# The last 65 keys of an attention kernel: their values and their scores made with the keys as the moving operand

## The chip, the cores and the metric

The kernel runs on one core of a Trainium2 chip. The metric is device time in microseconds; lower is better. TensorE is called PE here, VectorE DVE, ScalarE ACT, GpSimd POOL and SyncE SP, as the profile names them. On PE a matmul has a stationary operand, which a weight load (PEld) puts into the array, and a moving operand, whose columns are streamed through it.

## The reference

A gated cross-attention block followed by a mixture of low-rank adapters, all in fp32. There are 4 batches of 256 queries with 512 features, and a context of 1601 keys with 512 features. 32 query heads share 8 key-value heads (4 query heads each), with 128 features a head.

```python
q = (query @ Wq + bq).reshape(B, L, NKV, G, HDIM)
k_, v_ = jnp.split(kv @ Wkv + bkv, 2, axis=-1)
...
scores = jnp.einsum('blkgd,bmkd->bkglm', q, k) * scale
attn = jax.nn.softmax(scores, axis=-1)
o = jnp.einsum('bkglm,bmkd->blkgd', attn, v).reshape(B, L, NHEAD * HDIM)
return o @ Wo + bo
...
x = x + jnp.tanh(g_xattn[0]) * xattn(_layernorm(x), ctx, ...)
x = x + jnp.tanh(g_ffn[0]) * ffn(_layernorm(x), ...)
```

1601 keys are 12 blocks of 128 and 65 more. The change is about those 65.

## The kernel before

**Groups.** The main loop (lines 1976 to 2028) goes over batch `b`, key-value head `h` and half `l` of the queries: 4 x 8 x 2 = 64 groups. A group has 128 queries of 4 heads, so 512 columns. Its scores are kept as keys (partitions) by 512 queries in tiles `p`, two key blocks in each: seven tiles, of which the first (`j` = 0) holds the 65 last keys alone, in the half `p[:, 0, :]`; its other half is unused. `pairs` is the list of the seven.

**Scores, softmax, values.** `score_unit` (line 1217) makes one tile's scores: for each block a matmul into one PSUM bank (line 1246, keys stationary, 512 query columns moving), an eviction by ACT (line 1255), and then `fold` (line 1169) on DVE takes the running maximum, from tile 2 on; the 65 keys enter it at line 1178. `softmax` (line 1268) spreads the maximum over the keys, subtracts it tile by tile on DVE (line 1285), takes the exponential on ACT (line 1288), and sums on DVE. `av_unit` (line 1321) multiplies a tile of exponentials by the values (line 1337), and `normalize` finishes. `run_group` (line 1783) interleaves the scores of the present group with the value products of the previous one, tile by tile.

**Projections.** Keys, values and queries of two heads at a time come from `pair_steps` (line 971), which computes 2 x 2 blocks with 7 products in place of 8. For the values, the 65 last keys are done apart by `tail` (line 1124): for each of the two heads four matmuls with the 65 context rows stationary (`rest`, 65 columns) and the weights moving (128 columns) give 65 x 128 values in PSUM, which ACT copies into the value tile `v` (line 1136). That is run for 15 of the 16 pairs; the first pair has its own code. The x steps (line 589) load and normalise the inputs of two batches and turn them for the query projection; they run once at the start and once more in the middle, for batches 2 and 3.

**Order.** The order of instructions on PE, DVE and ACT is written by the program itself. It keeps estimated clocks (`clock`) for PE ("now"), DVE and ACT, and a list of the times at which the eight PSUM banks come free (`free`, `bank`, `give`). `spend(ns)` moves PE's clock on and lets waiting pieces of DVE and ACT work start (`pump`); `vec` and `act` move theirs; `later` puts a piece into a queue; `fit` emits pieces that fit before a given time; `force` emits what something depends on. Projections are tasks with a due group (`Task`, `window`), done between the groups or in free places. All the estimated costs are numbers in the code: `mm_cost(n)`, `BLOCK_COST` = 224 ns for a 128 x 128 block, `TR_COST` = 108 ns for a transpose. DMAs are issued by SP and POOL in the order of the program.

Of the kernel before, what the change touches and what calls it, by code (L numbers as in the profile page):

```python
# [10 lines left out]
F32 = mybir.dt.float32  # L11
# [4 lines left out]
P = 128  # L16
NHEAD = 32
NKV = 8
HDIM = 128
G = NHEAD // NKV  # L20
# [7 lines left out]
def flamingo_kernel(  # L28
# [51 lines left out]
    nc = tc.nc  # L80
    B, L, D = x.shape
    LK = ctx_kv.shape[1]
    NC = D // P
# [5 lines left out]
    FULL = KT - 1 if rows[-1] < P else KT  # L89
# [4 lines left out]
    pairs = [tuple(range(i, min(i + 2, FULL))) for i in range(0, FULL, 2)]  # L94
# [6 lines left out]
    HK = FULL // 2 * P  # L101
    NSUB = -(-HK // 512)
    SUB = HK // NSUB
    REST = rows[-1] if FULL < KT else 0
# [8 lines left out]
    small = ctx.enter_context(tc.tile_pool(name="small", bufs=4))  # L113
# [4 lines left out]
    SEM = 200  # L118
# [3 lines left out]
    clock = {"now": 0.0, "v": 0.0, "a": 0.0, "hold": 0.0}  # L122
    free = [0.0] * NBANK
    done = {}
    queues = {q: deque() for q in ("sub", "oT", "so", "exp", "ln", "T", "norm", "turn", "sum", "low", "low_a")}

    def vec(ns, ready=None):

        clock["v"] = max(clock["v"], clock["now"] + SEM if ready is None else ready) + ns
        return clock["v"] + SEM  # L130

    def act(ns, ready=None):
        clock["a"] = max(clock["a"], clock["now"] + SEM if ready is None else ready) + ns
        return clock["a"] + SEM
# [58 lines left out]
    def fit(engine, until):  # L193

        while True:
            some = [
                (start_of(q[0]), i, q)
                for i, q in enumerate(queues.values())
                if q and q[0][0] == engine and start_of(q[0]) + q[0][1] <= until + FIT
            ]  # L200
            if not some:
                return
            take(min(some)[2])

    def spend(ns, ready=0.0):

        clock["now"] = max(clock["now"], ready) + ns
        pump(clock["now"])
        turn_more()

    def bank(name):
        free.remove(min(free))
        return ps.tile([P, 512], F32, tag="bank", name=name)

    give = free.append


    ident = const.tile([P, P], F32, name="ident")
# [29 lines left out]
    def mm_cost(n):  # L248

        return 2 * (max(n, P) / 1.2 + 2)  # L250

    TR_COST = 108
    BLOCK_COST = 224
# [331 lines left out]
    JOINT = 2  # L585
# [79 lines left out]
    def key_col(i):  # L665

        return HK if i == FULL else i * P + (REST if i * P >= HK else 0)
# [198 lines left out]
    qT_t, kT_t, v_t = {}, {}, {}  # L866
# [104 lines left out]
    def pair_steps(kind, b, hp, then=None):  # L971
# [4 lines left out]
        nm = f"{kind}_{b}_{hp}"  # L976
        h0 = 2 * hp
        banks = {}
        second = {}

        def a(slot, c):
            return w_t[kind, b, hp][:, slot, c, :]
# [139 lines left out]
            ]  # L1122

        def tail():
            bk = bank(f"pt{nm}")
            for f in range(2):
                for j, (cols, slot, c) in enumerate(tail_cols(f)):
                    nc.tensor.matmul(  # L1128
                        bk[:REST, f * HDIM : (f + 1) * HDIM],
                        cols,  # L1130
                        a(slot, c),
                        start=j == 0,
                        stop=j == NC - 1,
                    )
            for f in range(2):
                nc.scalar.copy(v_t[b, h0 + f][:REST, FULL], bk[:REST, f * HDIM : (f + 1) * HDIM])
                t = act(250)
            give(t)
            over()
# [19 lines left out]
        parts = [[step(i, s, n) for i in (1, 2, 6, 7, 5, 4, 3)] for s, n in cols]  # L1159
        if REST and not wide:  # L1160
            ready = [("T", "kv", b), ("w", kind, b, hp)]
            parts.append([(2 * NC * BLOCK_COST, ready, tail, True)])
        left = [sum(len(p) for p in parts)]
        return parts

# [51 lines left out]
    def score_unit(key, j):  # L1217

        b, h, l = key
        nm = "_".join(map(str, key))  # L1220
        free_p = 0.0
        if j == 0:
            p_t[key] = []
            acc_t[key] = pool.tile([P, 2, W], F32, tag="mx", name=f"mx_{nm}", bufs=1)
        if key == last and j > 0:

            if j == 1:
                flat = pool.tile([P, NC * 2 * HW], F32, tag="ctxT", name="p_last", bufs=1)
                late.extend(
                    flat[:, i * 2 * W : (i + 1) * 2 * W].rearrange("p (t w) -> p t w", t=2)  # L1230
                    for i in range(NPAIR - 1)
                )
            p = late.pop(0)
        else:

            if len(ring) >= NBUF:
                before, i = ring[-NBUF]
                free_p = force(("sum", before, max(i, min(NPAIR - FULL // 2 + 1, NPAIR - 1))))
            ring.append((key, j))
            p = pool.tile([P, 2, W], F32, tag="p", name=f"p_{nm}_{j}", bufs=NBUF)  # L1240
        p_t[key].append(p)
        for k, i in enumerate(pairs[j]):
            r = rows[i]
            spend(mm_cost(W), max(min(free), done.get(("qT", b, h), 0.0)))
            sc = bank(f"sc_{nm}_{i}")
            nc.tensor.matmul(  # L1246
                sc[:r, :],
                kT_t[b, h][:, key_col(i) : key_col(i) + r],
                qT_t[b, h][:, :, l * P : (l + 1) * P],
                start=True,  # L1250
                stop=True,
            )
            t = max(clock["now"] + SEM, free_p)
            fit("a", t)
            nc.scalar.copy(p[:r, k, :], sc[:r, :])  # L1255
            t = act(585, t)
            give(t)
        fit("v", t)
        ns = fold(acc_t[key], ALU.max, j, key)
        if ns:  # L1260
            vec(ns, t)

    acc_t, sum_t, late, ring = {}, {}, [], []
    last = (B - 1, NKV - 1, NL - 1)
# [437 lines left out]
    tasks = []  # L1702
# [273 lines left out]
    for hi, (b, h) in enumerate(heads):  # L1976
        pair, coming = (b, h // 2), next_pair(b, h // 2)
        nxt = heads[hi + 1] if hi + 1 < len(heads) else None
        for l in range(NL):
            now = hi * NL + l  # L1980
            cur = (b, h, l)
            if cur == last:
                break
            if (h, l) == (NKV - 4, 1) and b + 1 < B and (b + 1) % JOINT == 0:
                load_pair("q", b + 1, 0)
                tasks.append(Task(x_steps(b + 1), now + 7))
            swap_at["group"] = now
            run_group(cur, prev)
            if prev is not None:
                steps = out_steps(prev)  # L1990
                if steps:
                    tasks.insert(0, Task(steps, now + 1 if by_blocks(*prev[:2]) else None))
                    if by_blocks(*prev[:2]):
                        out_task[prev[:2]] = tasks[0]
            prev = cur
            if (b, h, l) == (B - 1, NKV - 3, NL - 1):
                tail_space()
                tasks.append(Task(ffn_weight_steps() + [(0, 0, early_norms)]))
                both = [ffn_steps(*t) for t in early]
                tasks[:0] = [Task(route, now + 4) for route, _ in both]  # L2000
                tasks.extend(Task(steps, spare=True) for _, steps in both)
            if nxt is not None and nxt[0] % JOINT == 0:
                tasks.append(Task(q_steps(*nxt, l), now, first=True))
            elif nxt is not None and l == 0:
                load_q(*nxt)
            if coming is not None and (h % 2, l) == (0, 1):
                cb, cp = coming
                if cb == b:
                    then = lambda c=coming: next_weights("v", *c)
                    steps = sum(pair_steps("k", cb, cp, then), [])  # L2010
                else:
                    steps = first_k_steps(cb)
                tasks.append(Task(steps, (hi | 1) * NL + (NL - 1) * (cb == b), now))
            if coming is not None and (h % 2, l) == (1, 0):
                cb, cp = coming
                follow = next_pair(cb, cp)
                then = None if follow is None else lambda f=follow: next_weights("k", *f)
                for part in pair_steps("v", cb, cp, then):
                    tasks.append(Task(part, (hi | 1) * NL + NL, now))
                if cb == b and cp == NKV // 2 - 1 and b + 1 < B:  # L2020
                    tasks.append(Task(ctx_steps(b + 1)))
            if (h, l) == (NKV - 1, NL - 1) and b + 1 < B:

                force(("T", "kv", b + 1))
                force(("w", "v", b + 1, 0))
            window(now)
            if l == NL - 1 and nxt == heads[-1]:
                load_wo(*nxt)
# [51 lines left out]
```

## Time and profile before

| | us |
|---|---|
| median of 3 runs | 2532.07 (2532.05 to 2533.65) |
| the profiled execution | 2532.2 |
| its span | 2530.4 |
| PE busy | 2521.6 |
| DVE busy | 2175.3 |
| ACT busy | 1263.6 |
| POOL busy | 208.8 |

The granted PE clock is 1.00. The groups that hold most of the time, with the number of instructions and the mean of one:

| line, engine | what | count | busy us | mean ns |
|---|---|---|---|---|
| 1246 PE | scores of full blocks | 1536 passes | 720.6 | 592 |
| 1246 PE | scores of the 65 last keys | 128 passes | 65.3 | 592 |
| 1337 PE | value products | 1640 passes | 765.5 | 592 |
| 1128 PE | values of the 65 last keys | 240 passes | 31.1 | 273 |
| 1255 ACT | evictions of scores | 820 | 478.4 | 586 |
| 1255 ACT | of these, 65 keys | 64 | 37.2 | 581 |
| 1288 ACT | exponentials | 442 | 422.3 | 990 |
| 1285 DVE | subtractions | 442 | 482.4 | 1136 |
| 1136 ACT | evictions of the values' tail | 30 | 6.4 | 262 |

An fp32 matmul appears as two weight loads and two passes. Matmul ends are modelled and neighbours overlap, so the distance between two starts, or the chain's time over its count, says what a pass costs, and the mean duration doesn't. "Idle before" is the time for which an engine had nothing to do before the instructions of a row, and behind the arrow stands what ended it.

### The profile page before, as it was taken

How to read it: one execution, taken by the hardware profiler on the slowest of the kernel's cores; microseconds unless marked ns; L12 is line 12 of the kernel's file. 1: busy time of each engine (PE TensorE's matmuls, PEld its weight loads, DVE VectorE, ACT ScalarE, POOL GpSimd, SP SyncE). 2: the span in 40 equal slices, each digit the busy share in tenths (PEclk: the TensorE clock that was granted, in tenths of full speed). 3: DMA queues.
4: the chain of work that ended last, by engine and by line, in shares of the span. 5: the costliest groups of instructions: out<-in, count | busy, mean ns of one | idle time of the engine just before them, and what ended most of it. 6: DMA issues, size and time to landing. Idle time of an engine off the chain costs nothing.

```text
span 2530.4 us, 27018 instructions
## 1 busy us (share of the span) xinstructions
PE 2521.6 (100%) x9199; PEld 1493.8 (59%) x9199; DVE 2175.3 (86%) x3323; ACT 1263.6 (50%) x2062; POOL 208.8 (8%) x271
## 2 busy tenths in 40 slices
PE   9999999999999999999999999999999999999999
PEld 7557566565555656555665565756656565555544
DVE  4999898898899989999878887878788888889886
ACT  2545454545455554555545454545455455555551
POOL 1000000001001000110010000000000100000100
PEclk9999999999999999999999999999999999999999
DMA  5646857669666543224255535455532222221211
GB/s 170 143 92 130 146 123 118 151 110 246 80 92 99 85 81 74 71 71 152 58 98 100 98 77 96 109 81 110 154 80 65 82 54 67 67 63 44 71 34 50
DMA packets 300136, 246.24 MB, mean 97 GB/s; under 512 B 180533, under 2 KB 256341, under 8 KB 296158
## 3 DMA queue, kind: packets, MB, share of 16 engines
q1 hardware_dynamic: 267278, 211.71, 36.6%
q0 software_dynamic: 32192, 32.55, 8.8%
q8 instruction: 72, 1.18, 0.2%
q14 instruction: 66, 0.54, 0.1%
q10 hardware_dynamic: 528, 0.26, 0.0%
HBM read 147.96 MB, written 96.49 MB: 97 GB/s over the span
## 4 chain that ended last, share of the span: by engine, by line
PE 98%; DVE 1%; DMA 0%; ACT 0%; issue 0%; SPq 0%; ACTq 0%
PE sc L1246 28%; PE av L1337 27%; PE pxv L1015 6%; PE pxk L1004 6%; PE pxq L1004 4%; PE pox L472 4%; PE pyv L1015 3%; PE pyk L1004 3%; PE pyq L1004 2%; PE poy L472 2%; PE pzv L1015 2%; PE pzk L1004 2%; PE pzq L1004 1%; PE ptv L1128 1%; PE poz L472 1%; PE py L1581 1%
## 5 line engine op out<-in xcount | busy, mean ns | idle before, releaser
L1246 PE MATMUL sc<-qT,kT 128*128 128x512 f32 (+1 forms) x1664 | 775.9, 592 | 0.0
L1337 PE MATMUL av<-p,v 65*128 65x512 f32 x1640 | 765.5, 592 | 0.5 <-ACT p L1288 0.5
L1255 ACT COPY p<-sc 65x512 f32<-65x512 f32 x820 | 478.4, 586 | 572.8 <-PE sc L1246 549.0
L1337 PEld LDWEIGHTS av<-p,v 65*128 65x128 f32 x1640 | 311.2, 190 | 384.3 <-issue 380.1
L1246 PEld LDWEIGHTS sc<-qT,kT 128*128 128x128 f32 (+1 forms) x1664 | 308.1, 186 | 375.6 <-issue 349.5
L1285 DVE TENSOR_TENSOR p<-p,mb 65x512 f32<-65x512 f32 x442 | 482.4, 1136 | 0.3
L1288 ACT ACTIVATE p<-p 65x512 f32<-65x512 f32 x442 | 422.3, 990 | 31.0 <-DVE p L1285 29.7
L1181 DVE TENSOR_TENSOR mx<-mx,p 128x1024 f32<-128x1024 f32 x252 | 308.1, 1223 | 146.3 <-ACT p L1255 141.7
L478 POOL DMA_DIRECT2D kept_x<-po x210 | 182.6, 925 | 2039.8 <-ACT po L477 1864.4
L1181 DVE TENSOR_TENSOR sm<-sm,p 128x1024 f32<-128x1024 f32 x252 | 307.6, 1221 | 42.0 <-ACT p L1288 32.0
L1004 PE MATMUL pxq<-xq,wq 128*128 128x256 f32 x512 | 131.2, 379 | 0.0
L1049 ACT ACTIVATE kT<-pxk,biasT 128x384 f32<-128x384 f32 (+1 forms) x120 | 58.1, 509 | 126.5 <-PE pxk L1004 126.0
L1004 PEld LDWEIGHTS pxq<-xq,wq 128*128 128x128 f32 x512 | 92.4, 189 | 32.1 <-issue 15.8
L1049 ACT ACTIVATE qT<-pxq,biasT 128x256 f32<-128x256 f32 x64 | 30.4, 474 | 148.8 <-PE pxq L1004 148.8
L1175 DVE TENSOR_TENSOR mx<-p,p 128x1024 f32<-128x1024 f32 x63 | 76.9, 1221 | 31.6 <-ACT p L1255 31.4
L1004 PE MATMUL pxk<-T,wk 128*128 128x417 f32 (+1 forms) x240 | 90.4, 499 | 0.0
L1015 PE MATMUL pxv<-wv,ctxT 128*128 128x128 f32 x720 | 90.2, 275 | 0.0
L1015 PE MATMUL pxv<-wv,T 128*128 128x128 f32 x720 | 90.2, 275 | 0.0
L1004 PE MATMUL pxk<-ctxT,wk 128*128 128x417 f32 (+1 forms) x240 | 90.0, 499 | 0.0
L1015 PEld LDWEIGHTS pxv<-wv,ctxT 128*128 128x128 f32 x720 | 86.4, 192 | 4.2 <-issue 3.8
L1015 PEld LDWEIGHTS pxv<-wv,T 128*128 128x128 f32 x720 | 86.4, 192 | 4.2 <-issue 3.8
L1052 ACT COPY v<-pxv 128x384 f32<-128x384 f32 x90 | 43.0, 478 | 83.4 <-PE pxv L1015 83.1
(273 smaller groups left out, 2779.5 us busy)
## 6 DMA issues: line engine op xcount, KB each, us to landing
kept_x<-po POOLq DMA_DIRECT2D x210, 128.0 KB, 4.8
wo<-kept_wo SPq DMA_DIRECT2D x22, 1024.0 KB, 7.8
kept_q<-wq SPq DMA_DIRECT2D x16, 896.0 KB, 4.3
wq<-kept_q SPq DMA_DIRECT2D x16, 896.0 KB, 5.1
space<-kept_wo SPq DMA_DIRECT2D x22, 512.0 KB, 3.9
wk<-kept_k SPq DMA_DIRECT2D x11, 896.0 KB, 4.8
wv<-kept_v SPq DMA_DIRECT2D x11, 896.0 KB, 4.6
ctxT<-kept_ctx SPq DMA_DIRECT2D x12, 801.0 KB, 11.8
```

Of the source, the lines that this page charges most:

```text
L472: nc.tensor.matmul(bk[:, :HD], left[i]()[:, c, :], blk[:, c, :], start=first and c == 0, stop=c == 1, skip_group_check=True,)
L478: nc.gpsimd.dma_start(x2_kept[b, l, d], part, accum_op=ALU.add)
L1004: nc.tensor.matmul(bk[:, :n], a(SLOT[i], c), operand(i, c, s, n), start=first and c == 0, stop=c == 1, skip_group_check=True,)
L1015: nc.tensor.matmul(bk[:, t * HDIM : (t + 1) * HDIM], operand(i, c, s + t * P, P), a(SLOT[i], c), start=first and t == 0 and c == 0, stop=c ...
L1049: nc.scalar.activation(dst, src, AF.Identity, bias=bias_of(kind, h0 + f))
L1175: nc.vector.tensor_tensor(acc, p[first], p[first + 1], op)
L1181: nc.vector.tensor_tensor(acc, acc, p[j], op)
L1246: nc.tensor.matmul(sc[:r, :], kT_t[b, h][:, key_col(i) : key_col(i) + r], qT_t[b, h][:, :, l * P : (l + 1) * P], start=True, stop=True,)
L1255: nc.scalar.copy(p[:r, k, :], sc[:r, :])
L1285: nc.vector.tensor_tensor(p, p, m, ALU.subtract)
L1288: nc.scalar.activation(p, p, AF.Exp, scale=scale)
L1337: nc.tensor.matmul(av, v_t[b, h][:r, i, :], p_t[key][j][:r, k, :], start=(j == 0 and k == 0), stop=(j == NPAIR - 1 and k == len(pairs[j]) ...
```

## The change

It has three parts.

1. *Values.* `tail` now makes the weights stationary (128 columns) and the 65 context rows moving, so that PSUM holds 128 features x 65 keys for each of the two heads. ACT copies both into a new tile `vr` (128 x 130). A new step, `tail_turn`, transposes the two on PE into 65 x 128 and ACT copies these into `v` as before. The planner's cost for the tail's products goes from 224 to 124 ns each.
2. *Scores.* For tile 0, `score_unit` calls the new `score_rest`. Four matmuls, one for each query head, have the 128 queries stationary and the 65 keys moving; the result is 128 queries x 4 x 65 keys in one bank. DVE turns it in blocks of 32 x 32 out of PSUM into the unused half of the tile: the first 64 keys with one instruction, the last key, repeated 32 times, with another. ACT then places the blocks in twelve copies: for each of four strips of 32 queries two copies of 32 keys and one copy of the last key. These copies are emitted when the next tile's two evictions have been emitted. The rest of the softmax is as before.
3. *x steps.* For batches 2 and 3 they start when head 5 has reached its second half, in place of head 4, and are due 4 groups later in place of 7. Their loads move with them.

```diff
         def tail():
-            bk = bank(f"pt{nm}")
+            banks["t"] = bk = bank(f"pt{nm}")
             for f in range(2):
                 for j, (cols, slot, c) in enumerate(tail_cols(f)):
                     nc.tensor.matmul(
-                        bk[:REST, f * HDIM : (f + 1) * HDIM],
+                        bk[:, f * REST : (f + 1) * REST],
+                        a(slot, c),
                         cols,
-                        a(slot, c),
                         start=j == 0,
                         stop=j == NC - 1,
                     )
+            second["t"] = small.tile([P, 2 * REST], F32, tag="vr", name=f"vr_{nm}", bufs=1)
+            nc.scalar.copy(second["t"], bk[:, : 2 * REST])
+            done[nm, "t"] = act(230)
+            over()
+
+        def tail_turn():
+            bk = banks["t"]
             for f in range(2):
-                nc.scalar.copy(v_t[b, h0 + f][:REST, FULL], bk[:REST, f * HDIM : (f + 1) * HDIM])
+                nc.tensor.transpose(
+                    bk[:REST, (2 + f) * HDIM : (3 + f) * HDIM], second["t"][:, f * REST : (f + 1) * REST], ident
+                )
+            for f in range(2):
+                nc.scalar.copy(
+                    v_t[b, h0 + f][:REST, FULL], bk[:REST, (2 + f) * HDIM : (3 + f) * HDIM]
+                )
                 t = act(250)
             give(t)
             over()
...
-            parts.append([(2 * NC * BLOCK_COST, ready, tail, True)])
+            parts.append([(2 * NC * 124, ready, tail, True), (2 * TR_COST, (nm, "t"), tail_turn)])
...
         p_t[key].append(p)
+        if pairs[j] == (FULL,):
+            score_rest(key, p, free_p)
+            return
...
             give(t)
+        if key in turned:
+            t = turned.pop(key)(t)
         fit("v", t)
...
+    turned = {}
+
+    def score_rest(key, p, free_p):
+
+        b, h, l = key
+        assert REST == 65
+        spend(G * 2 * 62, max(min(free), done.get(("qT", b, h), 0.0)))
+        sc = bank(f"sr_{'_'.join(map(str, key))}")
+        for g in range(G):
+            nc.tensor.matmul(
+                sc[:, g * REST : (g + 1) * REST],
+                qT_t[b, h][:, g, l * P : (l + 1) * P],
+                kT_t[b, h][:, HK : HK + REST],
+                start=True,
+                stop=True,
+            )
+        by_key = sc[:, : G * REST].rearrange("p (g k) -> p g k", k=REST)
+        two = p[:, 1, : 2 * P].rearrange("p (g k) -> p g k", k=64)
+        one = p[:, 1, 2 * P : 3 * P].rearrange("p (g k) -> p g k", k=32)
+        t = max(clock["now"] + SEM, free_p)
+        fit("v", t)
+        nc.vector.transpose(two, by_key[:, :, :64])
+        nc.vector.transpose(one, by_key[:, :, 64:65].to_broadcast([P, G, 32]))
+        give(vec(600, t))
+        t = clock["v"] + SEM
+
+        def place(after):
+            dst = p[:, 0, :].rearrange("p (g q) -> p g q", g=G)
+            for a in range(4):
+                q, k = slice(32 * a, 32 * a + 32), 32 * a
+                for c in range(2):
+                    nc.scalar.copy(dst[32 * c : 32 * c + 32, :, q], two[q, :, 32 * c : 32 * c + 32])
+                nc.scalar.copy(dst[64:65, :, q], one[k : k + 1])
+            return max(after, act(12 * 220, t))
+
+        turned[key] = place
...
-            if (h, l) == (NKV - 4, 1) and b + 1 < B and (b + 1) % JOINT == 0:
+            if (h, l) == (5, 1) and b + 1 < B and (b + 1) % JOINT == 0:
                 load_pair("q", b + 1, 0)
-                tasks.append(Task(x_steps(b + 1), now + 7))
+                tasks.append(Task(x_steps(b + 1), now + 4))
```

## The prediction

> **What bounds the kernel now.** I read the page's busy times first, then the chain that ended last, then the groups with shapes kept apart, and then short stretches of chain and timeline.
>
> ```profile
> span 2530.4 us, 27018 instructions
> PE 2521.6 (100%) x9199; PEld 1493.8 (59%) x9199; DVE 2175.3 (86%) x3323; ACT 1263.6 (50%) x2062; POOL 208.8 (8%) x271
> PE 98%; DVE 1%; DMA 0%; ACT 0%; issue 0%; SPq 0%; ACTq 0%
> ```
>
> TensorE is never without work: 2521.6 of 2530.4 us, and the chain is 98% PE. A gain must come out of PE's own time; ScalarE (half idle) and VectorE (14% idle) can be loaded further until they make PE wait. So the question is what a PE pass costs. Every fp32 matmul stands in the trace as two weight loads and two passes. These rows are from the chain in two short stretches, and from the groups by shape:
>
> ```profile
> 246.87 1.75 PE ptv L1128 x16
> 1257.44 1.34 PE pxv L1015 x12
> L1246 PE MATMUL sc<-qT,kT 128*65 128x512 f32 x128 | 65.3, 592 | 0.0
> L1015 PEld LDWEIGHTS pxv<-wv,ctxT 128*128 128x128 f32 x720 | 86.4, 192 | 4.2 <-issue 3.8
> L1128 PEld LDWEIGHTS ptv<-wv,rest 128*65 128x65 f32 x180 | 20.1, 138 | 0.0
> ```
>
> Both products move 128 columns. With 65 stationary columns a pass takes 1.75/16 = 109 ns, with 128 it takes 1.34/12 = 112 ns. So at 128 x 128 it is no longer the moving operand that sets the pace but the weight load, which takes 54 ns more for 63 more columns (192 against 138). The start of a stream, where nothing hides the load, shows its length (timeline):
>
> ```profile
> 2391.28 0.41 PE L259 MATMUL pt_base<-ident,base 8*128 8x8 f32 x4
> 2391.61 0.30 PEld L1246 LDWEIGHTS sc<-qT,kT 128*128 128x128 f32 x2
> 2391.61 1.13 PE L1246 MATMUL sc<-qT,kT 128*128 128x512 f32 x2
> ```
>
> Two loads of 0.19 cover 0.30, so the second began 0.11 after the first: a full fp32 weight load holds the path 107 to 110 ns.
>
> **PE, part by part.** A 512-column pass takes 429 ns (four in 1.88 us in the timeline, the last one 0.592 long: (1.88 - 0.59)/3). Today the 65 last keys' scores are one matmul, 2 x 429 = 858 ns. The change moves the 65 keys against 128 stationary queries, four times: 8 passes, each with a full weight load. At 112 ns that is 896 ns: +38 ns in each of 64 groups, +2.4 us. The values' tail swaps its operands too: 16 passes go from 109.4 to 112 (1750 to 1792 ns), and two transposes are added at 109 ns (four of 128 columns take 0.60 us, the last 0.27). That is +260 ns in 15 pairs, +3.9 us. PE's sum is +6.3 us.
>
> No row shows a pass of 65 moving columns under 128 stationary ones, and 752 of them are added (64 x 8 + 15 x 16). Below, it cannot be cheaper than its columns: from 128 to 512 columns a pass grows by (429 - 109)/384 = 0.83 ns a column, so 65 columns cost 57 ns; the 8-column transposes above, about 70 ns apart ((0.41 - 0.20)/3), are near that, but their loads last 140 ns in the groups where fp32 products' last 192. Above, load and stream one after the other are 107 + 57 = 164 ns. Against 112 this is -41 and +39 us, so PE's sum lies between -35 and +45 us. I take 112, because the load already sets the pace at 128 x 128, and fewer moving columns do not shorten a load.
>
> The Trainium skill's page "TensorE: Matmul & The Clock Gate" has a rule for each side. Its section "Back-to-back issue gap" prices an isolated pass by the moving columns alone, 65/2.4 + 2.5 = 30 ns, and by it the sum would be an estimated -55 us. Its section "LDWEIGHTS (loading the stationary operand)" says that a load takes the stationary operand's column count over 1.2, so 107 ns here, and that speaks against the change: by it the sum would be about +3 us. The 112 against 109 ns above is the row that decides between them.
>
> **VectorE.** Each group gains two block transposes out of PSUM, of 256 and 128 elements.
>
> ```profile
> L718 DVE STREAM_TRANSPOSE swap<-ctx 128x256 f32<-128x256 f32 x72 | 27.7, 420 | 0.0
> ```
>
> 420 ns, and some 0.2 to 0.3 for half of it, make 0.65 us; 64 times, 42 us, and VectorE stands at 87.6% of the span. The tightest stretch has room:
>
> ```profile
> 832.50:905.40 72.90, 72.90 (x266) 41.92 (x265) 70.06 (x109) 38.51 (x63) 6.02 (x7) 1.00 0.51 79
> ```
>
> There VectorE is busy 70.06 of 72.90 us, and two groups add 1.3. Behind a transpose that waits for its product stand the subtractions of the group before, then ScalarE's exponentials, then PE's value products. I cost this at nothing while PE keeps its lead over those products (below).
>
> **ScalarE.** One eviction of 0.59 us goes; twelve copies of 128 elements come, after the two evictions of pair 1 and before those of pair 2. The only copies of this size from SBUF follow each other by 0.21 us:
>
> ```profile
> 6.14 0.30 ACT L860 COPY ctxT<-rest 128x128 f32<-128x128 f32 x1
> 6.35 0.30 ACT L862 COPY ctxT<-rest 128x132 f32<-128x132 f32 x1
> ```
>
> So they are 2.5 us at best and 12 x 0.30 = 3.6 without overlap; 2.5 is the nearer, since they stand in a row. Net it is about +2.0 us a group, +130 us, and ScalarE goes to 55%. In the group at 1228.9 it idles 1.19 us there, so pair 2's evictions come 1.3 us later, hold two banks longer, and push the first maximum (VectorE had idled 2.18 us for it); the 1.48 us of idle before the next maximum take that up. What the delay can cost is an exponential of the group before that stands behind the twelve copies. Reading the timeline from the end of each exponential to the product that reads it, in all 64 groups, nine have one that ends later than 3 us into the scores with under 5.5 us to spare: 0.83 (796.5), 0.83 (1179.1), 1.27 (2405.1), 3.41 (2437.7), 4.27 three times, 5.13 twice. The group at 2405.1:
>
> ```profile
> 2405.07 2.74 PE L1246 MATMUL sc<-qT,kT 128*65 128x512 f32 x6
> 2408.33 3.90 ACT L1288 ACTIVATE p<-p 128x1024 f32<-128x1024 f32 x4
> 2410.66 1.88 PE L1337 MATMUL av<-p,v 128*128 128x512 f32 x4
> ```
>
> A delay of 2.5 us is more than the slack in three. In the built order of the changed kernel the exponential in question stands ahead of the copies at 796.5 and 1179.1, and behind them at 2405.1: 2.5 - 1.27 = 1.2 us of PE waiting.
>
> **The x steps, moved.** The norms of the next two batches start two groups later and are due one group earlier. SP's loads (a pair of query weights, four tiles of x) and POOL's (the bias, then eight stores of x) move with them, past SP's issues of wv, qT and wo between 1078 and 1116 us. SP waits there for its next issue most of the time, and the first reader, the query projection at 1250.8, still stands behind all of it: nothing. On VectorE three tiles of about 2.9 us (statistics 0.68, norm 0.54, eviction 0.69, bias 0.74, small ones) move into 1117 to 1229 us, which has 7.4 us free; what does not fit meets 11.5 free us in the group at 1228.9. On ScalarE the square roots now stand singly among exponentials: 17 table loads against 13, at 1.283 us. One, with its root 1.5 us, stands ahead of pair 2's evictions at 1179.1, where five exponentials already run in a row; I put all 1.5 us down as PE waiting for banks.
>
> **The sum.** 6.3 + 1.2 + 1.5 = +9.0 us. The profiled execution took 2532.2 us (2530.4 of span and 1.8 around it), and the median shown is 0.1 lower: 2541 us.
>
> **Rivals.**
> - *The passes cost their moving columns (57 to 65 ns).* For it: the 8-column transposes at about 70 ns under 128 stationary columns. Against it: 112 against 109, and the 0.30 above. It turns into a gain below some 104 ns a pass (6.3/752 = 8 ns under 112). At 62 ns: 752 x -50 = -37.6, with the +6.3 it is -31, and with the waits 2.7, 2504 us. This is the other side.
> - *ScalarE's twelve copies become the wait.* If they take 3.6 us and start 2.4 us late, behind two of VectorE's subtractions (1.2 each), exponentials come 6 us later; the nine slacks then fall short by 5.2, 5.2, 4.7, 2.6, 3 x 1.7 and 2 x 0.9, together 24.6. With PE's 6.3: 2563 us. It decides from a delay over 2.5 us. For it: the load is wholly new and stands in one engine's order. Against it: 55 of 64 groups have over 5.5 us of slack.
> - *Nothing measurable:* passes at 104 to 108 ns and no waits, 2533. Against it: the row itself is 112.
> - That the change is not in the program is excluded: its built order has four 128x65 products and twelve copies in each of 64 groups.
>
> **How the numbers follow.** The forecast has 0.58, cheap passes 0.18, the ScalarE wait 0.16, no change 0.08. The forecast's own range is 2535 to 2549. The range is 2529 to 2570: it takes in no change and the ScalarE wait, leaves out the cheap passes (0.18) and some 0.02 above, where loads in series (+45 us) would lie. The measurement can tell about 0.2%, 5 us, from no change, so up to 2537 counts as the same: 0.08 of the forecast and the 0.08 of no change. Faster 0.18, same 0.16, slower 0.66.
>
> **What would show it.** In the changed profile the eight score passes of a group should take 0.90 us on the chain, the sixteen value passes 1.79, and the weight loads before them still 190 ns; at 0.50 and 1.0 us the first rival is right. ScalarE's twelve copies should take 2.5 us. PE's idle time should grow by under 4 us, most of it in the groups that begin near 1180 and 2405; over 20 us of it, behind exponentials or evictions, is the second rival.

## The result, and the profile after

| | before | after |
|---|---|---|
| median of 5 runs each, us | 2532.07 | 2553.01 (2552.63 to 2555.09) |
| profiled execution, us | 2532.2 | 2552.9 |
| span, us | 2530.4 | 2551.1 |

The changed kernel takes 1.0083 times as long (95% interval 1.0071 to 1.0094): 20.9 us more. The first lines of its page and its chain:

```profile
span 2551.1 us, 28660 instructions
PE 2531.1 (99%) x9613; PEld 1534.4 (60%) x9613; DVE 2205.8 (86%) x3451; ACT 1439.8 (56%) x2785; POOL 208.8 (8%) x271
PE 95%; DVE 2%; ACT 2%; DMA 1%; issue 0%; SPq 0%; DVEq 0%; ACTq 0%
```

PE's busy time grew by 9.5 us, and its idle time from 8.8 to 20.0 us, by 11.2. The chain used to be 98% PE; 3% of it has gone to DVE and ACT. The ends of matmuls are modelled, and a pass that starts after a wait shows up longer, so the starts tell it better. Adding up, over all passes, what lies between one start and the next beyond the pass's own length, where that is over 60 ns, gives 9.4 us before and 24.0 after: 14.6 of the 20.7 us of span are stoppages, and 6.1 are PE's passes. (Where the granted clock falls, the slowed passes count among the stoppages; in these two profiles it does not fall before the kernel's end.)

What a pass costs shows in two stretches of the chain, one with the eight score passes of a group and one with the sixteen value passes (start, length, what), and in the groups by shape:

```profile
205.63 1.73 PE ptv L1128 x16
...
1324.44 0.84 PE sr L1290 x8
1325.28 1.77 PE sc L1262 x4
```

```profile
L1290 PE MATMUL sr<-kT,qT 128*128 128x65 f32 x512 | 64.1, 268 | 0.0
L1290 PEld LDWEIGHTS sr<-kT,qT 128*128 128x128 f32 x512 | 65.9, 192 | 5.3 <-issue 0.3
```

0.84 is one pass of 55 ns, whose load was hidden behind the product before it, and seven of 112; the score product that follows takes those 55 ns more (1.77 us for four passes in place of 1.72), so a group pays 0.89 us where it paid 0.86. In most groups nothing else changed: they are 0.03 to 0.04 us longer each. Two neighbouring groups with a values' tail are together 0.28 to 0.33 longer, of which the tail makes 0.21 to 0.26.

Where the waits are shows in a table of three stretches of the program (columns: busy us and instructions of PE, PEld, DVE, ACT, POOL, then the granted clock, the DMA share and GB/s). The stretches run from the first group to the 34th, from there to the last but one, and to the end; first before, then after:

```profile
61.60:1312.20 1250.60, 1249.48 (x4568) 741.36 (x4567) 1127.60 (x1739) 643.22 (x1042) 99.28 (x121) 1.00 0.55 111
1312.20:2405.10 1092.90, 1092.90 (x3994) 646.49 (x3993) 919.52 (x1339) 555.08 (x903) 96.80 (x116) 1.00 0.38 83
2405.10:2530.40 125.30, 120.40 (x347) 57.62 (x345) 98.18 (x186) 47.67 (x75) 4.54 (x6) 1.00 0.15 42
```

```profile
62.00:1324.30 1262.30, 1255.34 (x4782) 762.15 (x4782) 1143.97 (x1803) 734.95 (x1416) 99.47 (x121) 1.00 0.55 110
1324.30:2418.60 1094.30, 1094.30 (x4170) 664.13 (x4169) 928.03 (x1392) 631.84 (x1226) 96.86 (x116) 1.00 0.37 83
2418.60:2551.10 132.50, 122.82 (x371) 59.69 (x369) 103.76 (x198) 55.35 (x101) 4.32 (x6) 1.00 0.13 40
```

The stretches grew by 11.7, 1.4 and 7.2 us. In the middle one VectorE is busy 84 to 85% of the time, and there PE does not wait at all: 1094.30 of 1094.30. In the first, VectorE is busy 90% before and 91% after, and PE's idle time goes from 1.1 to 7.0 us. In the last, the waits grow from 4.9 to 9.7. The 86% of the page hides this: it is an average over a stretch with slack and one nearly without. Slack is not the only difference, though: the newly loaded Wo blocks, of which more below, stand in the first stretch alone.

PE's waits in the changed kernel (us in all, times, longest); before, they were 0.5, 0, 0 and 0.6 us:

```profile
PE av L1392 <- ACT p L1343: 5.9, 4, 2.7
PE pxq L1004 <- DVE qs_q L1059: 2.7, 2, 2.2
PE sc L1262 <- ACT p L1271: 2.0, 4, 0.6
PE pox L472 <- DVE space L450: 1.4, 1, 1.4
```

Two thirds of these 12.0 us, 7.9, are for ScalarE. Its twelve copies, by shape and on the chain of the group that begins at 2418.6:

```profile
L1312 ACT COPY p<-p 32x128 f32<-32x128 f32 x512 | 151.5, 296 | 5.4 <-DVE p L1302 0.2
L1313 ACT COPY p<-p 1x128 f32<-1x128 f32 x256 | 75.4, 295 | 2.9
```

```profile
2421.39 0.59 ACT p L1271
2421.98 0.19 ACT p L1312
...
2422.18 0.30 ACT p L1312
...
2422.49 0.29 ACT p L1313
...
2425.26 0.29 ACT p L1313
...
2425.56 1.06 ACT p L1343
...
2426.67 1.98 PE av L1392 x4
```

Each copy starts 0.31 us after the one before, and the exponential (line 1343) that PE's value product needs stands behind all twelve: from the eviction's end to 2425.56 it is 3.6 us, and PE waits 2.73.

The other waits go back to VectorE. One of them begins far from where it is felt. Before (timeline of DVE), a group's maxima are folded (lines 1175, 1178) and then a newly loaded Wo block is combined (line 424):

```profile
214.94 1.22 DVE L1175 TENSOR_TENSOR mx<-p,p 128x1024 f32<-128x1024 f32 x1 [0.40 <-ACT p L1255]
216.20 0.69 DVE L1178 TENSOR_TENSOR mx<-mx,p 65x512 f32<-65x512 f32 x1
216.81 0.68 DVE L424 TENSOR_TENSOR space<-wo 128x512 f32<-128x512 f32 x1
```

After, in the same group:

```profile
216.93 0.71 DVE L1224 STREAM_TRANSPOSE sm<-sm 128x512 f32<-128x512 f32 x1
222.47 0.69 DVE L424 TENSOR_TENSOR space<-wo 128x512 f32<-128x512 f32 x1 [4.82 <-DMA wo<-in_L_xattn_Wo_dram]
223.19 1.42 DVE L424 TENSOR_TENSOR space<-wo,space 128x512 f32<-128x512 f32 x2
224.53 1.22 DVE L1188 TENSOR_TENSOR mx<-p,p 128x1024 f32<-128x1024 f32 x1
```

The program's own planner counts on the Wo block 6 us after the load's issue (`LAG_PAIR` = 6000 ns) and here puts its subtractions ahead of the fold. This load was issued at 211.38 and lands 11.1 us later. VectorE takes its instructions in order, and so the fold waits 4.82 us for a transfer that it does not need. That happens 6 times, 21.2 us in all; before, VectorE never waited for this load. In this group VectorE is still behind at 242.2, where PE waits for it (2.2 us in the list above, 2.4 from start to start).

### The profile page after: what moved, and what is told of

Its sections match the earlier page's. It is cut to its first block, busy times and chain, and to the rows that moved or that the text cites. A ratio compares the mean times of both kernels' runs of the same rounds, so it can differ in the third digit from the quotient of the medians.

```text
span 2551.1 us, 28660 instructions
## 1 busy us (share of the span) xinstructions
PE 2531.1 (99%) x9613; PEld 1534.4 (60%) x9613; DVE 2205.8 (86%) x3451; ACT 1439.8 (56%) x2785; POOL 208.8 (8%) x271
## 4 chain that ended last, share of the span: by engine, by line
PE 95%; DVE 2%; ACT 2%; DMA 1%; issue 0%; SPq 0%; DVEq 0%; ACTq 0%
PE av L1392 27%; PE sc L1262 24%; PE pxk L1004 6%; PE pxv L1015 6%; PE pxq L1004 4%; PE pox L472 4%; PE pyk L1004 3%; PE pyv L1015 3%; PE pyq L1004 2%; PE poy L472 2%; PE sr L1290 2%; PE pzk L1004 2%; PE pzv L1015 2%; PE pzq L1004 1%; PE ptv L1128 1%; PE poz L472 1%
## 5 line engine op out<-in xcount | busy, mean ns | idle before, releaser
L1262 PE MATMUL sc<-qT,kT 128*128 128x512 f32 x1536 | 724.2, 594 | 2.0 <-ACT p L1271 2.0
L1271 ACT COPY p<-sc 128x512 f32<-128x512 f32 x756 | 425.6, 587 | 395.0 <-PE sc L1262 352.1
L1262 PEld LDWEIGHTS sc<-qT,kT 128*128 128x128 f32 x1536 | 284.6, 190 | 332.7 <-issue 301.5
L1312 ACT COPY p<-p 32x128 f32<-32x128 f32 x512 | 151.5, 296 | 5.4 <-DVE p L1302 0.2
L1004 PEld LDWEIGHTS pxq<-xq,wq 128*128 128x128 f32 x512 | 92.3, 189 | 35.3 <-issue 14.6
L1188 DVE TENSOR_TENSOR sm<-p,p 128x1024 f32<-128x1024 f32 x63 | 76.8, 1218 | 17.0 <-ACT p L1343 15.9
## 6 DMA issues: line engine op xcount, KB each, us to landing
ctxT<-kept_ctx SPq DMA_DIRECT2D x12, 801.0 KB, 11.1
```

The source lines that it names most:

```text
L1004: nc.tensor.matmul(bk[:, :n], a(SLOT[i], c), operand(i, c, s, n), start=first and c == 0, stop=c == 1, skip_group_check=True,)
L1188: nc.vector.tensor_tensor(acc, p[first], p[first + 1], op)
L1262: nc.tensor.matmul(sc[:r, :], kT_t[b, h][:, key_col(i) : key_col(i) + r], qT_t[b, h][:, :, l * P : (l + 1) * P], start=True, stop=True,)
L1312: nc.scalar.copy(dst[32 * c : 32 * c + 32, :, q], two[q, :, 32 * c : 32 * c + 32])
```

## The experiments

Every ratio is to the kernel before, run beside it on the same chip (its medians were 2532.2 to 2532.8 us).

| kernel | median us | ratio, 95% interval |
|---|---|---|
| values alone | 2538.05 | 1.0020 [1.0011, 1.0028] |
| scores alone | 2555.49 | 1.0092 [1.0076, 1.0107] |
| x steps alone | 2533.75 | 1.0006 [0.9997, 1.0015] |
| PE's part alone | 2542.45 | 1.0039 [1.0027, 1.0052] |
| all, x steps back | 2576.17 | 1.0171 [1.0157, 1.0185] |
| two copies for twelve | 2552.80 | 1.0079 [1.0065, 1.0093] |
| true costs in the planner | 2549.00 | 1.0065 [1.0051, 1.0079] |
| 64 stationary queries | 2558.90 | 1.0103 [1.0089, 1.0117] |
| 128 moving columns | 2553.33 | 1.0081 [1.0065, 1.0096] |
| Wo combined later | 2554.36 | 1.0087 [1.0073, 1.0100] |
| Wo later and two copies | 2547.68 | 1.0060 [1.0048, 1.0073] |
| Wo later, x steps back | 2565.87 | 1.0130 [1.0114, 1.0147] |

**One part at a time.** First the values' tail alone: the scores of the 65 keys and the place of the x steps stay as before.

```diff
-        if pairs[j] == (FULL,):
-            score_rest(key, p, free_p)
-            return
-            if (h, l) == (5, 1) and b + 1 < B and (b + 1) % JOINT == 0:
+            if (h, l) == (NKV - 4, 1) and b + 1 < B and (b + 1) % JOINT == 0:
...
-                tasks.append(Task(x_steps(b + 1), now + 4))
+                tasks.append(Task(x_steps(b + 1), now + 7))
```

> The values' tail with its operands swapped and two transposes, alone; scores and x steps as before. Theory (PE time is the weight loads, the rest of the loss is waiting behind the score change's ScalarE copies): 15 pairs x 0.26 us = +3.9, so 2536 us, no new waits. Rival A (the values' new step, a round trip over ScalarE, causes waits too): 2540 us or more.

2538.05, 5.4 us more: between the theory's 2536 and rival A's 2540, and not without a new wait. Its span is 5.9 us longer, and its stoppages grew by 2.1 (11.5 against 9.4), with one new wait of 3.0 us for VectorE's sums of a head's output (`pox` for `space`, line 450) at 1103.5. That leaves 3.8 for the tail's passes.

Then the scores alone, with the old tail and the old place of the x steps:

```diff
-            banks["t"] = bk = bank(f"pt{nm}")
+            bk = bank(f"pt{nm}")
...
-                        bk[:, f * REST : (f + 1) * REST],
-                        a(slot, c),
                         cols,
+                        a(slot, c),
...
-            parts.append([(2 * NC * 124, ready, tail, True), (2 * TR_COST, (nm, "t"), tail_turn)])
+            parts.append([(2 * NC * BLOCK_COST, ready, tail, True)])
```

> The scores' change alone, with its transposes and twelve copies; values and x steps as before. Theory: +2.4 us of PE time and about 12 us of the new waits, so 2546 us. Rival B (the waits come from the x steps' new place): +2.4 and at most 5 us of waits, 2539 us or less.

2555.49, 22.9 us more, for 2.4 us of PE's own time: far over the theory's 2546, so rival B (2539 or less) is out, but the waits are more than the theory had. PE waits 8.3 us for the sums of line 450 (6.7 of it at 1113.4), 2.7 for an exponential, 2.1 for an eviction. So nearly all of the loss sits in the scores, and nearly all of that is waiting.

The x steps' move alone, in the kernel before:

```diff
-            if (h, l) == (NKV - 4, 1) and b + 1 < B and (b + 1) % JOINT == 0:
+            if (h, l) == (5, 1) and b + 1 < B and (b + 1) % JOINT == 0:
...
-                tasks.append(Task(x_steps(b + 1), now + 7))
+                tasks.append(Task(x_steps(b + 1), now + 4))
```

> The x steps in their new place, alone. Theory: within 2 us of 2532. Rival B: 2537 us or more.

2533.75: not to be told from no change. One new wait stands in the trace, 1.2 us for an exponential at 1183.5, where the prediction had put 1.5 us.

The three parts measured alone add up to 5.4 + 22.9 + 1.2 = 29.5 us, 8.6 more than together. They are not independent; the next run shows how much so.

**The x steps back in their old place, all else changed.** The diff is that of the x steps in the first kernel of this section.

> Values and scores changed, the x steps in their old place. Theory: the two parts alone add up (+5.4 and +22.9), 2559 to 2562 us, with a wait of several us for VectorE's block sums near 1110 us; the x steps' move is then worth some 7 us to the whole change. Rival (the x steps' move costs time): 2550 us or less.

2576.17: 23 us slower than with the move, and neither the 2559 to 2562 of the theory nor the rival's 2550 or less. So the rival is out, but not all of the 23 us is the x steps' doing. Up to 1029 us both programs give PE, VectorE and ScalarE the same instructions in the same order, and there the one with the x steps back already lags 13.1 us, of 24.5 at the end of the two profiles. The last experiment shows where most of these 13.1 us arise.

**PE's part alone.** PE does its new passes and transposes, but two evictions by ScalarE stand in place of VectorE's transposes and the twelve copies.

```diff
-        fit("v", t)
-        nc.vector.transpose(two, by_key[:, :, :64])
-        nc.vector.transpose(one, by_key[:, :, 64:65].to_broadcast([P, G, 32]))
-        give(vec(600, t))
...
+        fit("a", t)
+        nc.scalar.copy(p[:REST, 0, : G * REST], sc[:REST, : G * REST])
+        nc.scalar.copy(p[:REST, 0, G * REST :], sc[:REST, : W - G * REST])
+        t = act(700, t)
+        give(t)
```

> All three parts, but of the scores' change only PE's products: two ScalarE evictions of the bank's first 65 partitions stand in for the transposes and the twelve copies, so that the 65 keys' scores are not the reference's. Theory: PE's +6.3 us and almost no new waits, 2539 us. Rival (the waits come from the planner's too cheap PE costs or from the x steps): 2546 us or more.

2542.45, 9.9 us more, between the theory's 2539 and the rival's 2546. Its span is 10.2 us longer and its stoppages grew by 4.6 (14.0 against 9.4; waits of 3.3 us for line 450 and of 2.4 for exponentials are in them), so 5.6 are left for PE's passes. 11.0 of the 20.9 us appear only once VectorE's transposes and ScalarE's copies are there.

**What a pass costs.** Half the stationary columns (VectorE then turns 64 partitions, and the copies place the first 64 queries' scores twice), and then twice the moving ones:

```diff
-                sc[:, g * REST : (g + 1) * REST],
-                qT_t[b, h][:, g, l * P : (l + 1) * P],
+                sc[:64, g * REST : (g + 1) * REST],
+                qT_t[b, h][:, g, l * P : l * P + 64],
```

> The whole change with 64 stationary queries in place of 128 in the 65 keys' products; the second 64 queries of each head get the first ones' scores, so they are not the reference's. Theory (the weight load sets the pace of a pass): 55 to 62 ns a pass in place of 112, 0.4 us less PE time a group, 2527 to 2535 us. Rival (a pass costs 112 ns for another reason): 2553 us.

```diff
-                sc[:, g * REST : (g + 1) * REST],
+                sc[:, g * P : (g + 1) * P],
                 qT_t[b, h][:, g, l * P : (l + 1) * P],
-                kT_t[b, h][:, HK : HK + REST],
+                kT_t[b, h][:, HK : HK + P],
```

> The changed kernel with 128 moving columns instead of 65 in each of the 512 turned score products (the columns beyond the 65 hold other keys' scores and are not used); the order and all else stay. Theory (a pass is as long as the load of its 128 stationary columns, 112 ns measured from start to start): 128 columns cost 109 ns of their own, so the passes stay at 109 to 115 ns, and the time stays within 3 us of 2553. Rival (65 columns were what a pass paid for, on top of a fixed part): 53 ns more a pass, 512 of them, 27 us, 2580 us.

The chain of each, in a group without waits, with the product that follows, first with 64 stationary columns, then with 128 moving ones:

```profile
1539.76 0.61 PE sr L1290 x8
1540.37 1.91 PE sc L1262 x4
```

```profile
1323.20 0.89 PE sr L1290 x8
1324.09 1.72 PE sc L1262 x4
```

128 moving columns cost nothing (2553.33 against 2553.01): the eight passes take 0.89 us, each 112 ns; only the first, whose load is hidden, grows from 55 to about 110, and the product that follows is as much shorter (1.72 against 1.77). With 64 stationary columns a pass among the eight starts 58 ns after the one before (median of the starts), in place of 112. So the weight load sets the pace of a 65-column pass under 128 stationary columns, as the prediction had it. With half the load, the load (by estimate half of 107 to 110 ns) and the stream (65 columns at 0.83 ns, so 54) are too near each other to tell which one sets it.

A group gains much less from this than the 0.4 us that were expected. On the chain the eight passes and the product after them take 0.61 + 1.91 us in place of 0.84 + 1.77: 0.09 us less, 5.6 in 64 groups. By the starts, the product ahead of the eight takes 93 ns more, the eight 609 ns, and the one behind 104 ns more, together 806 against 893. The time is lost at the change from products with 128 stationary columns to 64 and back. The values' tail of the kernel before has 65 stationary columns among products with 128 and loses nothing there (109 ns from its first pass to its last), so why 64 do is open.

The time went the other way: 2558.90, neither the theory's 2527 to 2535 nor the rival's 2553. The instructions stand in the same order as in the changed kernel, but VectorE waits 29.2 us for the Wo load in place of 21.2, and PE 9.6 us for the next pairs' queries in place of 2.7. So the expectation was right about a pass, wrong about what a group gains, and it left out the waits.

**ScalarE's copies.** Two copies of 384 and 128 columns stand in place of the twelve. The planned time falls with them, and the plan orders all three engines anew.

```diff
-            for a in range(4):
-                q, k = slice(32 * a, 32 * a + 32), 32 * a
-                for c in range(2):
-                    nc.scalar.copy(dst[32 * c : 32 * c + 32, :, q], two[q, :, 32 * c : 32 * c + 32])
-                nc.scalar.copy(dst[64:65, :, q], one[k : k + 1])
-            return max(after, act(12 * 220, t))
+            nc.scalar.copy(p[:REST, 0, : 3 * P], p[:REST, 1, : 3 * P])
+            nc.scalar.copy(p[:REST, 0, 3 * P :], p[:REST, 1, :P])
+            return max(after, act(700, t))
```

> The whole change, but two ScalarE copies (of 384 and of 128 columns) in place of the twelve, so that the 65 keys' scores are not the reference's; PE's products and VectorE's transposes stay. Theory (ScalarE's 3.7 us of copies are what most of the new waits stand behind): the waits for exponentials and evictions near 1197, 2427 and 2465 go, 2545 us. Rival (VectorE's transposes and its order): 2550 us or more.

PE's waits for ScalarE are gone, but the time is 2552.80, no different, and the rival's 2550 or more holds. What took their place:

```profile
PE pox L472 <- DVE space L450: 6.0, 1, 6.0
PE pxq L1004 <- DVE qs_q L1059: 4.7, 3, 2.3
```

**The planner's costs** set to what the trace shows:

```diff
-        spend(G * 2 * 62, max(min(free), done.get(("qT", b, h), 0.0)))
+        spend(G * 2 * 112, max(min(free), done.get(("qT", b, h), 0.0)))
-        give(vec(600, t))
+        give(vec(680, t))
-            return max(after, act(12 * 220, t))
+            return max(after, act(12 * 308, t))
```

(and the tail's cost from 124 to 224 ns a block.)

> The whole change with the planner's costs set to what the trace shows (112 ns for a pass, 224 for a value product, 308 for a copy, 680 for the transposes). Theory (the copies cost ScalarE time whatever the order): 2548 to 2554 us. Rival (the waits are the planner's errors): 2542 us or less, that is PE's own +6.3 us and little more.

2549.00, inside the theory's 2548 to 2554 and above the rival's 2542; that is 4 us below the changed kernel, with intervals that overlap. Waits remain at other places (2.05 us at 2458, 1.84 at 2510.7). Wrong estimates are a part of the loss at most.

**The Wo blocks out of VectorE's way.** One number is altered: their combinations are planned 5 us later.

```diff
-                "T", "v", 700, clock["now"] + LAG_PAIR,
+                "T", "v", 700, clock["now"] + LAG_PAIR + 5000,
```

> The changed kernel with one number altered: the four subtractions that turn a newly loaded Wo block into its combinations (line 424, VectorE) are planned 5 us later after the load's issue. The whole computation is kept. In the profile after, VectorE stands still in front of them 6 times, 21.2 us in all, until the load has landed (in the profile before: not once for the load), because the planned pause of VectorE in front of the first fold of a group's maxima has grown by the copies' planned time and the planner puts them into it. Theory (VectorE, held up by a transfer, is what made PE wait at 81.8 and 242.2 us): the 21.2 us of VectorE's waits for the load fall below 3 us, PE's waits for the queries of the next pair (2.7 us in all) fall below 0.5, and the time falls by 3 to 5 us, to about 2549 us. Rival (VectorE has the room there and something else would hold PE at the same places): VectorE's waits for the load go, PE's waits stay at 2 us or more, and the time stays within 2 us of 2553.

VectorE's waits for the load fall from 21.2 to 2.6 us and the 2.4 us at 242.2 are gone, as the theory had it. The time is not better: 2554.36, as the rival had it. The 0.6 us at 81.8 stay (now at 82.9), so the load was not what PE waited for there. PE now waits 1.1 us for queries at 491.4 and 0.5 to 0.7 at two more places, and in the profiled execution two waits at 2427 and 2467 us, which the changed kernel has as well, each cost 1.5 to 1.7 us more (below). By itself this run does not settle it.

What brought the subtractions ahead of their load is open. The expectation names the copies' planned time, and the runs do not bear that out. VectorE waits 16.2 us for this load (5 times) with the values changed alone and 10.7 (4 times) with PE's part alone, and neither has the copies; it waits 22.7 us where two copies are planned at 700 ns in place of 2640, and only 8.1 where twelve are planned at 3696 (the true costs). What is shown is that the plan relies on 6 us, that the loads take 6.1 to 11.1 us in the changed kernel (6.1 to 9.8 before), and that planning the subtractions later ends all but 2.6 us of the waits.

Both eased together:

> The changed kernel with both suspected waits eased: the Wo block's subtractions are planned 5 us later, and two copies of ScalarE (384 and 128 columns) stand in place of the twelve; the scores of the last 65 keys are then not in their places. With two copies alone the waits for ScalarE at 1197, 2427 and 2465 us were gone, but PE waited 4.7 us for the queries and 6.0 us at 1188 us for VectorE's sums, and the time stayed at 2552.8. Theory (the queries' waits come from the load in VectorE's way, ScalarE's from the twelve copies): the 4.7 us go, the wait at 1188 us stays or moves, and the time is 2545 to 2549 us. Rival (what is taken away in one place is given back at another by VectorE, which has 29 us more to do whatever the copies are): 2551 us or more, with new waits for VectorE of 5 us and over.

2547.68, inside the theory's 2545 to 2549 and below its rival's 2551. The waits for queries are 0.5 us instead of 4.7 and those for exponentials 0.2. What is left is mostly one wait: 6.0 us for line 450 at 1180.9, where the x steps' work stands among VectorE's own just ahead of it; no run tests whether that is the reason.

Last, the same number altered where the stake was largest, with the x steps in their old place. The expectation asked for 2562 to 2567 by the theory, and within 3 us of 2576 by its rival.

> The changed kernel with the x steps in their old place (2576 us without more) and the Wo block's subtractions planned 5 us later. The whole computation is kept. With the x steps back alone VectorE stood 30.5 us before those subtractions and PE waited 11.1 us for the next pair's queries, at 243.8, 332.4 and 502.3 us, long before any x step. Theory (those three waits come from the load that stands in VectorE's way, and have nothing to do with the x steps): VectorE's waits for the load fall below 4 us, PE's waits for the queries below 2 us, and the time falls by 9 to 14 us, to 2562 to 2567; the waits for ScalarE (7.4 us) and for VectorE's sums at about 1127 us (5.9) stay. Rival (as with the x steps moved, where the same edit took 2.4 us of waits away and the time stayed at 2554): PE waits as long at other places and the time stays within 3 us of 2576.

2565.87, 10.3 us less. PE's and VectorE's waits, first with the x steps back alone:

```profile
PE pxq L1004 <- DVE qs_q L1059: 11.1, 4, 4.6
DVE space L424 <- DMA wo<-in_L_xattn_Wo_dram: 30.5, 6, 7.2
```

and with the Wo blocks later as well:

```profile
PE pxq L1004 <- DVE qs_q L1059: 2.7, 2, 2.3
DVE space L424 <- DMA wo<-in_L_xattn_Wo_dram: 3.8, 1, 3.8
```

The waits at 243.8 and 332.4 us are gone, long before any x step. The third is not: the same pass waits at 490.9, 2.4 us from start to start where it was 2.9, and there VectorE has just stood 3.8 us, at 476.2, before the one load that still comes late. So the 2.7 us left are more than the 2 that the theory allowed, but they point the same way. With the Wo blocks later in both, the x steps' move is worth 11.5 us (2565.87 against 2554.36). So of the 23 us between x steps moved and x steps back, some 10 to 12 belong to the Wo load; the rest stands at 1115.9 (a wait of 5.7 us for line 450, which the move avoids) and in what follows such waits. One thing stays open: why the load of 222 us lands 13.4 us after its issue with the x steps back and 11.1 with them moved, in the same order of issues. In both, the DMA share is 1.08 to 1.35 from 210 to 220 us, and two thirds of the packets from 200 to 226 us are under 512 B.

No version here beats the kernel before: the PE part alone costs more than it gives.

## Why the prediction was right, and where it was not

The direction and the range held: 2553 lies between 2529 and 2570, though 12 us above the forecast of 2541 and outside the forecast's own 2535 to 2549. That the range takes it in is in part luck: it reaches so far up for a rival, 24.6 us of waits behind ScalarE, and the waits that came were fewer there and in part behind VectorE. Step by step:

- *PE, +6.3 us.* Right. The passes take 112 ns, a group pays 0.03 to 0.04 us (0.038 was predicted), a values' tail 0.21 to 0.26 (0.26). The lower price of 57 ns by the columns is excluded at 128 stationary columns, and with it the rival of cheap passes. So are the 30 ns that the prediction took from the Trainium skill's page "TensorE: Matmul & The Clock Gate", section "Back-to-back issue gap". That page's section "LDWEIGHTS (loading the stationary operand)" gives 107 ns and is near the measured 112.
- *ScalarE's copies, 2.5 us, 1.2 us of waiting.* The term was mis-sized. The price of 0.21 us came from two neighbouring copies at the kernel's start; twelve in a row do not overlap, 0.31 apart, 3.7 us, the "3.6 without overlap" that the prediction named and did not take. With the slack of 1.27 at 2405.1 that alone makes 2.4 us there (the view shows 2.73). The copies also delay evictions (2.0 us) and the last group. In all it is 7.9 us of waits, not 1.2.
- *VectorE, 0.65 us a group, nothing.* This step failed, not in its price (450 and 274 ns were measured, 0.65 us from start to end) but in "I cost this at nothing". Two things were missing. VectorE also waits for the product it transposes: 27.3 us in 44 times. And in the new plan VectorE stands 21.2 us before work that waits for a DMA. The check of room (70.06 of 72.90 us) counted busy time alone; what a late VectorE costs shows where it stands in front of PE: 2.7 us for queries and 1.4 for line 450 in the changed kernel, 6.0 us for line 450 in both runs with two copies.
- *The x steps, 1.5 us.* About right alone (1.2, within what can be told). What the prediction did not see is what the move avoids: it counted what moves into the stretch, not what leaves the place where block sums are due.
- *The idle time of PE under 4 us.* It grew by 11.2. That is neither the forecast nor the second rival (over 20); of the rival's mechanism, 3.6 us of copies came true, its 2.4 us of lateness did not (ScalarE waits 0.2 us in all for the transposes before its copies), so only a few of its nine slacks gave way.

So the sum fell short by its waits: 2.7 us were predicted and the stoppages grew by 14.6. Where they come from is shown for two of them: two copies in place of twelve end the waits for ScalarE, and the Wo blocks planned later end the 2.4 us at 242.2. Both edits together take 5 us off the time and no more, because in the new order PE waits 6.0 us for line 450; what holds VectorE up there is read from its order and not tested. How the rest would divide can't be said, since each edit alone moved the time by less than 2 us and each changes the plan as well.

## What to carry to other kernels

Here an fp32 pass with 65 moving columns was as long as the load of its 128 stationary columns, 112 ns, so fewer moving columns gained nothing. With 64 stationary columns it took 58 ns, but most of that was lost again at the change from wide products to narrow ones and back. Before work is put on an engine "with 14% to spare", look at that engine's share stage by stage, and at whose instructions stand behind it in its order; an engine that executes in order makes all that stands behind a wait late, a DMA's wait too. And where a program plans its own order from estimated costs, a small change can move work ahead of the transfer that it needs: look at what the new plan has put before what. Lastly, before a difference is put down to an edit, look at where along the program it arises: here 13.1 us of it lay where both orders were the same.

## What the runs showed of the hardware

**A wait of PE can cost more than it lasts.** The same wait of 2.73 us before the same four value products, in two kernels (timeline of PE, and then the window that follows the wait, with the granted clock third from the end), first in the changed kernel:

```profile
2426.67 1.98 PE L1392 MATMUL av<-p,v 128*128 128x512 f32 x4 [2.73 <-ACT p L1343]
```

```profile
2426.60:2429.00 2.40, 2.33 (x6) 1.13 (x7) 2.22 (x4) 2.40 (x4) 1.10 (x2) 1.00 0.35 100
```

and with Wo combined later:

```profile
2427.49 3.53 PE L1392 MATMUL av<-p,v 128*128 128x512 f32 x4 [2.73 <-ACT p L1343]
```

```profile
2427.40:2429.00 1.60, 1.51 (x2) 0.84 (x3) 1.43 (x4) 1.60 (x3) 1.37 (x3) 0.50 0.27 85
```

1.98 us against 3.53: in the second the granted clock fell to 0.50, and passes of 429 ns took 853. In the thirteen profiles of changed kernels, measured from start to start beyond the pass's own length, PE stood still for 1.5 us or more 44 times. After the 9 waits up to 1.84 us the clock stayed; after 14 of the 24 between 2.05 and 2.92 it fell; after all 11 from 3.06 on it fell. The slow stretch then cost mostly 1.7 us more, up to about 3. The Trainium skill's page "TensorE: Matmul & The Clock Gate", section "HAM oscillation — how this bites in real kernels", warns of gaps of PE over about 3.4 us; here gaps of 2.05 already did it in some cases. So two kernels with nearly the same waits can differ: of the 2.7 us between the spans of these two, 1.8 arise here (two falls cost 1.6 and 1.7, and 1.4 come back at the next waits). With the x steps back the granted clock stood at 0.50 in six stretches, 23.9 us together, and the passes in them took some 11 us longer.

**The partitions of a copy cost nothing on ScalarE here.** A copy of 1 x 128 elements takes 295 ns, one of 32 x 128 takes 296, and one of 65 x 128 takes 296; the two long copies that replaced twelve (the other, 65 x 384, takes 511) ended the waits for ScalarE.
